# Scores, masks and shifts of an attention kernel as sixteen 32x32 tiles instead of four 32x128 tiles

## Chip, cores and metric

The kernel runs on one core of one Trainium2 chip. The metric is the device time of one execution in microseconds. The kernel before takes 2215.35 us, the median of three runs (2215.28 to 2217.46).

## The reference

Eight sequences of 1024 tokens with 512 features go through one gated attention layer, all in float32:

```
xn = layernorm(x)                                   # per token, no scale or offset
q, k, v = xn @ W.T + b                              # 16 heads of 32 features
scores  = q @ k.T / sqrt(32)                        # 1024 x 1024 per head
scores  = where(i % 256 >= j % 256, scores, -1e30)  # the mask repeats every 256
s   = softmax(scores) @ v @ Wo.T + bo
w   = +1 where weights >= 0 else -1
g   = silu(clip((xn @ w.T) * scale + bias, -100, 100))
out = x + s * g
```

## The kernel before, in words

**Order of the tokens.** Tokens are stored so that token `w * 256 + m` stands at place `4 * m + w`. The mask then depends on `m` alone, and a block of 128 places against a block of 128 places is either all kept, all masked (and left out), or on the diagonal, where a mask of 32 steps of 4 places is added.

**Sequences, groups, quads.** The main loop runs over 8 sequences `b`, 4 groups `g` of four heads, and 9 quads `n`: 288 steps. A quad is a PSUM tile of 128 partitions, 4 heads and 512 columns (one bank for each head). There is one quad buffer (`ps_q`, `bufs=1`), which two kinds of blocks use in turn:

- *Maxima* (`maxima_quad`, tile `s`, lines 513 and 525), for the group after the present one. Queries stand on the partitions, keys on the columns. Where the quad holds a diagonal block, a product of two bf16 constants (`place_of`, `after`, line 513) first puts the mask there. Then for each of the four heads a float32 product of 32 rows, the features of that head, adds the scores (line 525). VectorE takes the maximum over the keys (line 537).
- *Scores* (`probs_quad`, tile `t`, lines 592, 603 and 614), for the present group. Keys stand on the partitions, queries on the columns. First minus the maximum of each query is put on all 128 keys: a bf16 product of three rows, the three bf16 parts of the maximum, with a constant of -1 (line 592, `shift`). Then the mask (line 603) and the scores (line 614). ScalarE takes the exponential from the quad to SBUF (line 627).

The lists `S_QUADS` and `T_QUADS` say which blocks a quad holds: one segment of 512 columns, or two whose widths add up to 512 (128 and 384, or 256 and 256). Four of nine maxima quads and four of nine score quads have no mask.

**Tiles of TensorE.** A matmul uses as many rows of the array as its operands have partitions, and as many columns as its output has. In the quads each head's product is a tile of 32 rows and 128 columns (the shift: 3 rows of its 32), and the four heads lie side by side along the rows: `lhsT` and `rhs` start at partition `h * 32`, the output goes to the bank of head `h`. The names in the profile are 32*128 and 3*128. All other large products are tiles of 128 rows and 32 columns, four side by side along the columns: probabilities times values (`attend_quad`, line 640), the projections and the output (`product`, line 358), the sums of the probabilities (line 681) and the turn of the maxima (`shift_rows`, line 566). The gate (line 456) and the transposes (lines 259 and 328) use 128 by 128.

A float32 product is one instruction in the program and four on the engine: weight load, matmul, weight load, matmul. A bf16 product is one weight load and one matmul. So line 525 with one segment of 512 columns is 4 products, 8 matmuls, in two passes of four.

**What sets the order.** `tc.manual_schedule()` keeps the order in which the code issues. In each step it is: scores quad of this step (`probs_quad`), probabilities times values of the step before (`attend_quad`), a share of other work, the maxima quad of the next group (`maxima_quad`), and more other work. The other work (projections, gate, transposes, output) comes from a list for each group (`STEADY`, `OPENING`, `CLOSING`), where each piece has a cost written by hand; `fill` takes pieces until a wanted sum of costs is reached. The costs are constants in the code, not measured at run time.

## Time and profile before

| what | value |
|---|---|
| median of the runs | 2215.35 us |
| profiled execution, first to last instruction (span) | 2213.6 us |
| instructions in the span | 57362 |
| TensorE clock granted | 1.000 |
| DMA queues: instructions for TensorE (q8) | 203 packets, 3.33 MB |
| HBM read and written | 56.37 and 33.55 MB, 41 GB/s over the span |

The groups of the three kinds of quad work by shape (all four widths for the scores):

| line, shape | matmuls | mean ns of one | weight loads of the line, mean ns |
|---|---|---|---|
| 525 `s`, 32x512 float32 | 1536 | 632 | 184 |
| 614 `t`, 32x512 float32 | 1536 | 596 | 185 |
| 592 shift, 3x512 bf16 | 768 | 384 | 91 |
| 603 mask, 32x128 bf16 | 1024 | 215 | 93 |
| 513 mask, 32x256 bf16 | 384 | 278 | 91 |
| 640 `av`, 128x512 float32 | 1536 | 605 | 108 |

How to read it: the busy time of an engine is the union of its instructions' times, and matmuls that lie side by side overlap in it. Their ends are modelled. A mean of 632 ns is therefore not what a matmul takes from the engine; the distance between the starts of successive passes is. "PEld" are the weight loads, which run beside the matmuls. In a timeline, `x8` at the end of a line means that eight instructions were merged, and the second number is the time from the first start to the last end.

### The profile page before, as it was taken

How to read it: one execution, taken by the hardware profiler on the slowest of the kernel's cores; microseconds unless marked ns; L12 is line 12 of the kernel's file. 1: busy time of each engine (PE TensorE's matmuls, PEld its weight loads, DVE VectorE, ACT ScalarE, POOL GpSimd, SP SyncE). 2: the span in 40 equal slices, each digit the busy share in tenths (PEclk: the TensorE clock that was granted, in tenths of full speed). 3: DMA queues.
4: the chain of work that ended last, by engine and by line, in shares of the span. 5: the costliest groups of instructions: out<-in, count | busy, mean ns of one | idle time of the engine just before them, and what ended most of it. 6: DMA issues, size and time to landing. Idle time of an engine off the chain costs nothing. (4 is left out here: it accounts for less than half of the span.)

```text
span 2213.6 us, 57362 instructions
## 1 busy us (share of the span) xinstructions
PE 2182.9 (99%) x26015; PEld 857.3 (39%) x26015; DVE 1276.7 (58%) x1635; ACT 876.0 (40%) x862; POOL 1325.6 (60%) x1198
## 2 busy tenths in 40 slices
PE   8999999999999999999999999999999999999998
PEld 4334333333333443333333333334333443333333
DVE  4556556665557655566555665565655665555564
ACT  2235433444344444344443443434443343333332
POOL 1356565666566656576556665556765666755562
PEclk9999999999999999999999999999999999999999
DMA  4001000121001210012000120002200111000113
GB/s 167 2 16 35 11 7 30 54 73 35 25 25 40 73 35 25 25 59 72 16 25 25 63 68 16 25 25 68 63 16 25 45 59 63 11 21 25 44 54 125
DMA packets 49676, 93.60 MB, mean 42 GB/s; under 512 B 5388, under 2 KB 5656, under 8 KB 49432
## 3 DMA queue, kind: packets, MB, share of 16 engines
q1 hardware_dynamic: 48728, 88.76, 12.1%
q8 instruction: 203, 3.33, 0.6%
q10 hardware_dynamic: 704, 1.18, 0.2%
q14 instruction: 41, 0.34, 0.0%
HBM read 56.37 MB, written 33.55 MB: 41 GB/s over the span
## 5 line engine op out<-in xcount | busy, mean ns | idle before, releaser
L659 POOL TENSOR_TENSOR p<-p,p 128x512 f32<-128x512 f32 x930 | 1096.3, 1209 | 395.2 <-ACT p L627 242.9
L537 DVE TENSOR_REDUCE pm<-s 128x4 f32<-128x2048 f32 (+3 forms) x384 | 664.0, 1750 | 588.6 <-PE s L525 586.7
L627 ACT ACTIVATE p<-t 128x2048 f32<-128x2048 f32 x288 | 540.9, 1878 | 839.3 <-PE t L614 764.0
L715 DVE RECIPROCAL aT<-aT 128x128 f32<-128x128 f32 x256 | 230.3, 928 | 214.9 <-ACT aT L676 214.9
L525 PE MATMUL s<-k,q 32*128 32x512 f32 (+3 forms) x3072 | 315.3, 504 | 1.1 <-ACT q L401 0.8
L640 PE MATMUL av<-p,v 128*32 128x512 f32 (+3 forms) x3072 | 307.4, 495 | 1.6 <-DVE aT L719 1.4
L614 PE MATMUL t<-q,k 32*128 32x512 f32 (+3 forms) x3072 | 306.1, 492 | 0.0
L358 PE MATMUL k_ps<-xnT,wkT 128*32 128x512 f32 (+3 forms) x2832 | 254.9, 477 | 1.7 <-ACT wkT L274 0.7
L358 PE MATMUL q_ps<-xnT,wqT 128*32 128x512 f32 (+2 forms) x2656 | 254.1, 497 | 1.7 <-ACT shift L572 0.8
L358 PE MATMUL v_ps<-wvT,xnT 128*32 128x512 f32 (+3 forms) x2728 | 254.8, 489 | 0.0
L358 PE MATMUL o_ps<-woT,aT 128*32 128x320 f32 (+2 forms) x2568 | 243.9, 503 | 1.5 <-ACT shift L572 0.8
L741 POOL TENSOR_TENSOR s<-s,xb 128x512 f32<-128x512 f32 x63 | 86.3, 1370 | 212.3 <-DVE s L740 210.2
L358 PEld LDWEIGHTS k_ps<-xnT,wkT 128*32 128x32 f32 x2832 | 83.7, 109 | 169.0 <-issue 138.3
L614 PEld LDWEIGHTS t<-q,k 32*128 32x128 f32 x3072 | 139.1, 185 | 25.8
L358 PEld LDWEIGHTS q_ps<-xnT,wqT 128*32 128x32 f32 x2656 | 78.9, 109 | 174.0 <-issue 151.6
L640 PEld LDWEIGHTS av<-p,v 128*32 128x32 f32 x3072 | 70.3, 108 | 195.9 <-issue 163.4
L358 PEld LDWEIGHTS v_ps<-wvT,xnT 128*32 128x32 f32 x2728 | 79.2, 109 | 168.6 <-issue 143.5
L456 PE MATMUL y_ps<-fwT,x 128*128 128x512 f32 x464 | 135.5, 418 | 1.7 <-ACT k L401 1.3
L525 PEld LDWEIGHTS s<-k,q 32*128 32x128 f32 x3072 | 117.0, 184 | 52.0 <-ACT p L627 42.2
L358 PEld LDWEIGHTS o_ps<-woT,aT 128*32 128x32 f32 x2568 | 76.1, 109 | 151.4 <-issue 133.1
L429 POOL TENSOR_TENSOR x<-xnT,x 128x512 fp32r<-128x512 f32 x58 | 74.1, 1277 | 100.0 <-ACT x L428 100.0
L435 POOL TENSOR_SCALAR y<-y 128x512 f32<-128x512 f32 x64 | 39.6, 619 | 153.1 <-DVE y L434 101.3
(96 smaller groups left out, 1475.8 us busy)
## 6 DMA issues: line engine op xcount, KB each, us to landing
g<-t SPq DMA_DIRECT2D x64, 256.0 KB, 2.0
gb<-g SPq DMA_DIRECT2D x64, 256.0 KB, 2.9
xb<-in_L_attn_x_dram SPq DMA_DIRECT2D x64, 256.0 KB, 3.1
out_dram<-s SPq DMA_DIRECT2D x63, 256.0 KB, 2.5
x<-in_L_attn_x_dram SPq DMA_DIRECT2D x62, 256.0 KB, 3.1
wq_st<-in_L_attn_Wq_dram SPq DMA_DIRECT2D x2, 512.0 KB, 5.1
wv_st<-in_L_attn_Wv_dram SPq DMA_DIRECT2D x2, 512.0 KB
fw_st<-in_L_ffn_weights_dram SPq DMA_DIRECT2D x2, 512.0 KB, 9.7
```

Source lines behind the costliest of these rows:

```text
L358: nc.tensor.matmul(hold[0][cols, lo:hi], lhsT=lhsT[:, cols], rhs=rhs[:, lo:hi], start=(i == 0 and lo == 0), stop=(i == n - 1), skip_group_ ...
L429: nc.gpsimd.tensor_tensor(part[1], src, part[0].bitcast(F32), ALU.subtract)
L435: nc.gpsimd.tensor_scalar(y[0], y[0], MAX_VAL, -MAX_VAL, ALU.min, ALU.max)
L456: nc.tensor.matmul(hold[0], lhsT=part[i][:, c, :], rhs=wT["fw"][:, c, :], start=(i == 0 and c == 0), stop=(i == 1 and c == NC - 1),)
L525: nc.tensor.matmul(sc[:, h, at : at + w], lhsT=qt[b, g][head_rows(h), i * P : (i + 1) * P], rhs=kt[b, g][head_rows(h), lo:hi], start=(at = ...
L537: nc.vector.tensor_reduce(pm[:, 0 if lo == 0 else 1, i, :], sc[:, :, at : at + w], AX.X, ALU.max)
L614: nc.tensor.matmul(sc[:, h, at : at + w], lhsT=kt[b, g][head_rows(h), j * P : (j + 1) * P], rhs=qt[b, g][head_rows(h), q0 : q0 + w], start ...
L627: nc.scalar.activation(pt[:, :, :width], sc[:, :, :width], AF.Exp, scale=SCALE)
L640: nc.tensor.matmul(av[b, g, f][head_rows(h), lo : lo + w], lhsT=vt[b, j][:, g * P + h * DK : g * P + (h + 1) * DK], rhs=pts[b, g, n][:, h, ...
L659: nc.gpsimd.tensor_tensor(t[:, hs, lo : lo + w], t[:, hs, lo : lo + w], p[:, hs, at : at + w], ALU.add)
L715: nc.vector.reciprocal(r, r)
L741: nc.gpsimd.tensor_tensor(s, s, xr, ALU.add)
```

## The change

In `maxima_quad` and `probs_quad` every product of a head is split in four by its output partitions. `COLS` are the four slices of 32 columns of the array; each new product has 32 rows (3 in the shift) and 32 columns, takes 32 columns of `lhsT`, streams the same `rhs` as before, and writes 32 partitions of the head's bank. Heads are the outer loop, columns the inner one. Where there was a set of four products there is a set of sixteen. Operands, types, accumulation order and everything outside the two functions are as before.

```diff
+    COLS = [slice(c * DK, (c + 1) * DK) for c in range(NH)]
+    HEAD_COLS = [(h, c) for h in range(NH) for c in COLS]
...
                 rows_h = after[head_rows(h), :].unsqueeze(1)
-                nc.tensor.matmul(
-                    sc[:, h, :].rearrange("p (a t) -> p a t", t=P)[:, masked[0] :: step, :],
-                    lhsT=place_of[head_rows(h), :],
+                for c in COLS:
+                    nc.tensor.matmul(
+                        sc[c, h, :].rearrange("p (a t) -> p a t", t=P)[:, masked[0] :: step, :],
+                        lhsT=place_of[head_rows(h), c],
...
-            for h in range(NH):
+            for h, c in HEAD_COLS:
                 nc.tensor.matmul(
-                    sc[:, h, at : at + w],
-                    lhsT=qt[b, g][head_rows(h), i * P : (i + 1) * P],
+                    sc[c, h, at : at + w],
+                    lhsT=qt[b, g][head_rows(h), i * P + c.start : i * P + c.stop],
                     rhs=kt[b, g][head_rows(h), lo:hi],
...
-            for h in range(NH):
+            for h, c in HEAD_COLS:
                 r = slice(h * DK, h * DK + 3)
                 nc.tensor.matmul(
-                    sc[:, h, at : at + w],
-                    lhsT=neg1[r, :],
+                    sc[c, h, at : at + w],
+                    lhsT=neg1[r, c],
                     rhs=shift[b, g, f][r, lo : lo + w],
...
-                for h in range(NH):
+                for h, c in HEAD_COLS:
                     nc.tensor.matmul(
-                        sc[:, h, at : at + P],
-                        lhsT=after[head_rows(h), :],
+                        sc[c, h, at : at + P],
+                        lhsT=after[head_rows(h), c],
                         rhs=place_of[head_rows(h), :],
...
-            for h in range(NH):
+            for h, c in HEAD_COLS:
                 nc.tensor.matmul(
-                    sc[:, h, at : at + w],
-                    lhsT=kt[b, g][head_rows(h), j * P : (j + 1) * P],
+                    sc[c, h, at : at + w],
+                    lhsT=kt[b, g][head_rows(h), j * P + c.start : j * P + c.stop],
                     rhs=qt[b, g][head_rows(h), q0 : q0 + w],
```

More of the change, by code (lines that the diff above doesn't have):

```diff
@@ L512, in maxima_quad @@
                 rows_h = after[head_rows(h), :].unsqueeze(1)
-                nc.tensor.matmul(
-                    sc[:, h, :].rearrange("p (a t) -> p a t", t=P)[:, masked[0] :: step, :],
-                    lhsT=place_of[head_rows(h), :],
-                    rhs=rows_h.to_broadcast([MT, len(masked), P]),
-                    start=True,
-                    stop=False,
-                    skip_group_check=True,
-                )
+                for c in COLS:
+                    nc.tensor.matmul(
+                        sc[c, h, :].rearrange("p (a t) -> p a t", t=P)[:, masked[0] :: step, :],
+                        lhsT=place_of[head_rows(h), c],
+                        rhs=rows_h.to_broadcast([MT, len(masked), P]),
+                        start=True,
+                        stop=False,
+                        skip_group_check=True,
+                    )
         at = 0
```

## Prediction

> **What bounds the kernel now.** I read the page first. TensorE (PE) has work for 99% of the span at full clock, and no other engine passes 60%.

> ```profile
> PE 2182.9 (99%) x26015; PEld 857.3 (39%) x26015; DVE 1276.7 (58%) x1635; ACT 876.0 (40%) x862; POOL 1325.6 (60%) x1198
> ...
> PEclk9999999999999999999999999999999999999999
> ...
> q8 instruction: 203, 3.33, 0.6%
> ```

> The reader is to see that PE's own queue sets the end, that the clock hides nothing, and that 26015 matmuls and 26015 weight loads come in as 3.33 MB of instructions. Next I read the waits of PE alone, longest first:

> ```profile
> PE t L592 <- DVE pm L537: 4.2, 4, 1.5
> PE t L592 <- ACT p L627: 1.6, 5, 0.8
> ```

> These are the two longest, 5.8 us in all. PE waits for nobody, so whatever this change adds to or takes from PE goes straight into the time, and there is no cover. The diff touches no other engine: built, both programs have the same instructions in the same order on the other four queues, and the same waits and signals on PE.

> But a busy PE is not a PE at its peak, so the timeline comes third: not the durations, which are modelled and overlap, but the distance from one group's start to the next.

> ```profile
> 1000.58 0.40 PE L592 MATMUL t<-shift,neg 3*128 3x512 bf16 x4
> 1000.80 0.23 PE L603 MATMUL t<-place_of,after 32*128 32x128 bf16 x4
> 1000.86 1.08 PE L614 MATMUL t<-q,k 32*128 32x512 f32 x8
> 1001.88 1.07 PE L640 MATMUL av<-p,v 128*32 128x256 f32 x16
> 1002.76 1.05 PE L358 MATMUL k_ps<-xnT,wkT 128*32 128x192 f32 x16
> ```

> A float32 product runs as two passes, each of four matmuls side by side. av (1001.88 to 1002.76) streams 512 columns in two passes in 0.88 us; the scores (L614) need 1.02 us for the same. Where the maxima's scores have no mask in front it is worse:

> ```profile
> 1020.21 1.14 PE L525 MATMUL s<-k,q 32*128 32x512 f32 x8
> 1021.28 2.79 PE L358 MATMUL o_ps<-woT,aT 128*32 128x192 f32 x32
> ```

> That is 1.07 us. I therefore took the start of every PE instruction in the trace and subtracted the streaming time: 0.833 ns a column in float32, 0.417 in bf16, what steady runs show (128x32 passes of 512 columns repeat every 429 ns, a shift of 512 takes 0.22 us). Of 2207 us between PE starts 1940 is streaming; 267 is overhead. The 288 score blocks (T) and 288 maxima blocks (S) hold 580 us of streaming and 97.6 us of overhead inside them. Two things explain it:

> - *Leaving a tile size.* The last pass before another tile size lasts 107 ns longer after 32x128 tiles, 117 after 128x32, about 98 after a 128x128 transpose. Four tiles start one after the other, 3.6 ns apart with 32x128 and 6.6 ns with 128x32, so these are one number: 96 ns plus the lag of the last tile (3 x 3.6 = 11, 3 x 6.6 = 20).
> - *First weights.* Behind such a change the weights cannot be loaded early. The first pass then lasts 107 ns longer with 128 columns of float32 weights (S without mask), 27 with 32 columns (av). One mask pass in front hides about half of the 107.

> **The change, part by part.** In the built programs PE gains 4608 float32 products for each of L525 and L614 (two matmuls each), 4608 for the shift (L592), 3072 and 1920 for the masks (L603, L513). That is 18432 + 9600 = 28032 matmuls, and as many weight loads: 54047 of each after, 108094 instructions against 52030. The streamed columns stay: sixteen tiles stream at once where four did. That sixteen streams keep pace is not shown; four 128x32 tiles already cover the same 128 by 128 places, with a stream of their own each, at 429 ns a pass, so I cost it at nothing.

> 1. *First weights, less.* 32 columns to load instead of 128. Block overhead beyond the 107 of the exit, now and with 27 ns (13 for bf16, or behind a pass that covers the rest): S without mask 110 to 27, 128 blocks, 10.6 us; S with one mask 68 to 13, 64 blocks, 3.5; S in two segments 23 to 13, 96 blocks, 1.0; T with one mask 70 to 13, 64 blocks, 3.6; T in two segments 82 to 20, 96 blocks, 6.0; T without mask nothing. Sum: **-24.7 us**.
> 2. *Exit, more.* The last tile now lags by fifteen steps, not three. At 3.6 ns the exit is 96 + 54 = 150 (43 more), at 6.6 it is 96 + 99 = 195 (88 more). Times 576 blocks: +24.8 to +50.7 us. I take 6.6: twelve of fifteen steps go to another column of the array, and every row of the trace that does so has 6.6. **+50.7 us**.
> 3. *Narrow bf16 passes.* 384 passes (256 of masks in T, 64 in S, 64 of shifts) stream 128 columns in 53 ns and repeat every 57. Sixteen starts need 16 x 3.6 = 58 (nothing lost) or 16 x 6.6 = 106 (49 more each, 18.8 us). Same row, so **+18.8 us**.
> 4. *Feeding PE.* The trace has no long run as dense as the new blocks, so bounds. Below: nothing, if instructions come as fast as tiles start (3.3 ns each within a group now). Above: the densest 1000 starts of the trace took 33.4 us; if that were all PE can be fed, 108094 x 33.4 ns = 3610 us. The densest short runs are 32 starts in 0.22 us (7.0 each) and 64 in 0.69 us (10.8). Those are demands met, not limits, so I take **0** and keep the rest as a rival.

> Sum: -24.7 + 50.7 + 18.8 + 0 = +44.8 us on a span of 2213.6, 2258.4; the runs shown have 1.75 us more (median 2215.35), so **2260 us**. With 3.6 ns in 2 and 3 it would be +0.1, 2215: bounds 2215 to 2260 before item 4. What is late next is still PE; other engines' waits move with it. If the lag were covered (PE waiting elsewhere), items 2 and 3 would cost nothing, but only 5.8 us of such waits exist.

> [...] Matmuls on different tiles start 3.6 and 6.6 ns apart here. [...]

> **The rivals.**

> *A, the forecast*: only items 1 to 3 act, with a lag between 3.6 and 6.6 ns: 2205 to 2275. For it: the lag is visible at each group. Chance 0.45.

> *B, PE cannot be fed inside the blocks.* A T block in two segments would hold 256 instructions in 1.17 us, one each 4.6 ns, longer than any burst of the trace. At 7.0 ns: 96 such blocks lose 0.62 us each, 96 S blocks in two segments (160 instructions, 0.96 us) 0.16: 75 us, which with +44.8 gives 2335. At 10.8: 1.59 and 0.77 us each, 0.26 for 64 masked T, 0.13 for 64 masked S: 252 us, 2512. With the short lag the two are 2290 and 2467. Against it: PE shows no hole behind its densest bursts now. It decides from about 5 ns an instruction. I place it at 2275 to 2480, 0.31.

> *C, far slower*: PE is fed no faster than about 15 ns an instruction, or sixteen tiles stream as two sets of eight (580 us more). Up to 3610, 0.08.

> *D, the other side: no drain.* After the change every neighbour with 128x32 tiles has the same 32 columns. If PE drains only where the columns of a tile change, 479 entries (118 ns now) and 539 exits (107) fall to the 8 ns that a change of operands costs inside one tile size: 52.7 + 53.4 us, with item 1 another 24.7, so 2085; if only one side falls, about 2140; with a lag that eats part, up to 2205. Against it: 32x128 to 128x128 changes the rows alone and costs 105 ns. Chance 0.16.

> That the change does not do what it says is excluded by the built program.

> **How the numbers follow.** About 0.2% (4.4 us) is what a measurement of this kernel can tell from no change. A gives 0.06 faster (weights win, lag 3.6 or less), 0.08 same, 0.31 slower; B and C slower, D faster: 0.22 / 0.08 / 0.70. The range leaves out C (0.08) and the deeper part of D (0.11): 2170 to 2480. A alone: 2205 to 2275.

> **What would show it.** In the profile after: the same blocks, start to start. Item 1 is right if S without mask has a first pass near 454 ns instead of 534; item 2 if the last pass before another tile size is 150 to 195 longer than streaming; item 3 if mask passes repeat each 58 to 106 ns. B shows as holes between starts inside T blocks in two segments, where PE waits for nothing ("issue"), while plain S blocks stay good; D as exits near 8 ns. The instruction queue should carry about 6.9 MB. Wrong would be the whole sum if a float32 pass of sixteen tiles repeats at much more than 429 ns.

## The result, and the profile after

The changed kernel takes **2408.52 us**, the median of four runs (2407.01 to 2411.05); the kernel before, on the same chip, 2215.32 (2215.24 to 2217.46). The ratio is 1.0869, with a 95% interval of 1.0855 to 1.0883. The profiled execution has a span of 2406.3 us where the kernel before had 2213.6: +193. The forecast was 2260. The direction and the range held; of the size, 45 us out of 193 were foreseen.

The page of the changed kernel, by the lines that were read before:

```profile
PE 2374.5 (99%) x54047; PEld 977.2 (41%) x54047; DVE 1285.3 (53%) x1635; ACT 878.2 (36%) x862; POOL 1326.8 (55%) x1198
...
PEclk9999999999999999999999999999999999999999
...
q8 instruction: 422, 6.91, 1.2%
```

The work of the other engines is what it was (POOL 1326.8 us against 1325.6), the clock is full (1.0 granted), and the instruction queue carries the 6.91 MB that were expected. PE is "busy" for 99% here too, so this page alone does not say what it lost. The waits of PE don't either:

```profile
PE t L596 <- DVE pm L541: 3.1, 3, 1.3
PE xnT_ps L331 <- DVE x L315: 2.1, 2, 1.4
```

The longest is 3.1 us in total. But for such small sums PE still waits for nobody: the 193 us are its own. The timeline of PE shows where they are (start in us, time from the first start to the last end, line, operation, number of instructions):

```profile
1055.57 1.16 PE L529 MATMUL s<-k,q 32*32 32x512 f32 x32
1056.66 0.74 PE L361 MATMUL q_ps<-xnT,wqT 128*32 128x320 f32 x8
...
1059.38 0.43 PE L596 MATMUL t<-shift,neg 3*32 3x512 bf16 x16
1059.60 0.27 PE L607 MATMUL t<-place_of,after 32*32 32x128 bf16 x16
1059.79 1.29 PE L618 MATMUL t<-q,k 32*32 32x512 f32 x32
1061.01 1.06 PE L644 MATMUL av<-p,v 128*32 128x512 f32 x8
...
1067.45 0.44 PE L596 MATMUL t<-shift,neg 3*32 3x384 bf16 x32
1067.81 0.48 PE L607 MATMUL t<-place_of,after 32*32 32x128 bf16 x32
1068.08 1.49 PE L618 MATMUL t<-q,k 32*32 32x384 f32 x64
1069.50 1.07 PE L644 MATMUL av<-p,v 128*32 128x512 f32 x8
```

Take the distance from one start to the next. The maxima without mask (1055.57 to 1056.66) take 1.09 us, where they took 1.07. The scores with one mask (1059.38 to 1061.01) take 1.63, where they took 1.30: the shift keeps its 0.22, the mask takes 0.19 (was 0.06), the products 1.22 (was 1.02). The scores in two segments (1067.45 to 1069.50) take 2.05, where the kernel before takes 1.36 (1008.38 to 1009.74):

```profile
1008.38 0.40 PE L592 MATMUL t<-shift,neg 3*128 3x384 bf16 x8
1008.61 0.28 PE L603 MATMUL t<-place_of,after 32*128 32x128 bf16 x8
1008.72 1.09 PE L614 MATMUL t<-q,k 32*128 32x384 f32 x16
1009.74 0.64 PE L640 MATMUL av<-p,v 128*32 128x512 f32 x4
```

The same for all 576 blocks, with streaming subtracted as in the prediction. "Instructions" are weight loads and matmuls of PE in one block:

| block | number | instructions before, after | mean overhead before, ns | after, ns | difference, us |
|---|---|---|---|---|---|
| S, no mask | 128 | 16, 64 | 217 | 231 | +1.8 |
| S, one segment, mask | 64 | 24, 96 | 175 | 430 | +16.3 |
| S, two segments | 96 | 40, 160 | 130 | 634 | +48.4 |
| T, no mask | 128 | 24, 96 | 130 | 436 | +39.3 |
| T, one segment, mask | 64 | 32, 128 | 177 | 508 | +21.3 |
| T, two segments | 96 | 64, 256 | 188 | 871 | +65.6 |

Together that is 192.7 us, as much as the spans differ. One row stands apart: the block of 64 instructions is hardly slower, and every block of 96 or more is.

Inside a block the trace shows a stop. Here is the start of a score block without mask, cut off at 457.15 us:

```profile
456.88 0.44 PE L596 MATMUL t<-shift,neg 3*32 3x512 bf16 x16
457.09 0.62 PE L618 MATMUL t<-q,k 32*32 32x512 f32 x8
```

All sixteen tiles of the shift have started, but of the sixteen products only eight. Medians over the 128 blocks of this kind, in ns from the block's first start: the shift's tiles start at 0 to 50; the first eight products together at 226 to 250, as the shift ends; the ninth at 411, 185 ns after the first; the rest 16.7 ns apart until 528. The second pass repeats that stagger (first tiles at 659, last at 979), and the next group comes at 1496: the last tile's start, 427 of streaming, and 90. In the kernel before, such a block takes 1.18 us from start to start:

```profile
1024.00 0.39 PE L592 MATMUL t<-shift,neg 3*128 3x512 bf16 x4
1024.22 1.03 PE L614 MATMUL t<-q,k 32*128 32x512 f32 x8
1025.18 0.64 PE L640 MATMUL av<-p,v 128*32 128x512 f32 x4
```

### The profile page after: what moved, and what is told of

Its sections match the earlier page's. It is cut to its first block, busy times and chain, and to the rows that moved or that the text cites. A ratio compares the mean times of both kernels' runs of the same rounds, so it can differ in the third digit from the quotient of the medians.

```text
span 2406.3 us, 113426 instructions
## 1 busy us (share of the span) xinstructions
PE 2374.5 (99%) x54047; PEld 977.2 (41%) x54047; DVE 1285.3 (53%) x1635; ACT 878.2 (36%) x862; POOL 1326.8 (55%) x1198
## 3 DMA queue, kind: packets, MB, share of 16 engines
q8 instruction: 422, 6.91, 1.2%
q10 hardware_dynamic: 704, 1.18, 0.1%
## 5 line engine op out<-in xcount | busy, mean ns | idle before, releaser
L618 PE MATMUL t<-q,k 32*32 32x512 f32 (+2 forms) x12288 | 398.5, 489 | 0.5 <-issue 0.5
L529 PE MATMUL s<-k,q 32*32 32x512 f32 (+2 forms) x12288 | 381.7, 490 | 1.0 <-ACT q L404 0.8
L618 PEld LDWEIGHTS t<-q,k 32*32 32x32 f32 x12288 | 187.6, 103 | 39.2 <-issue 15.2
L529 PEld LDWEIGHTS s<-k,q 32*32 32x32 f32 x12288 | 145.3, 103 | 59.5 <-ACT p L631 39.7
```

The lines of the kernel that those rows point to most:

```text
L529: nc.tensor.matmul(sc[c, h, at : at + w], lhsT=qt[b, g][head_rows(h), i * P + c.start : i * P + c.stop], rhs=kt[b, g][head_rows(h), lo:hi] ...
L618: nc.tensor.matmul(sc[c, h, at : at + w], lhsT=kt[b, g][head_rows(h), j * P + c.start : j * P + c.stop], rhs=qt[b, g][head_rows(h), q0 : q ...
```

## Experiments

My theory after the result, **the queue**: PE takes in at most 64 instructions counted from the oldest that still streams. A bf16 tile is two of them, a float32 product four. A shift of sixteen tiles fills 32 places, eight products the other 32. Everything behind waits until the shift ends, then comes in at a rate of its own, and the exit waits for the last tile. Rivals: a **price for each instruction**, wherever it stands; the **fetch** of instructions from memory (q8); a limit on the number of **tiles or rows** that stream at once; the **tile size** itself.

### The order of the tiles

```diff
-    HEAD_COLS = [(h, c) for h in range(NH) for c in COLS]
+    HEAD_COLS = [(h, c) for c in COLS for h in range(NH)]
```

(and the same in the mask of the maxima)

> The changed kernel with the sixteen tiles of each set issued column by column (heads inside) instead of head by head. Queue theory (PE holds some 64 instructions ahead; those behind come at about 4.2 ns each, and after a full stop only some 185 ns later, so the second half of sixteen tiles starts late): the time stays, 2395 to 2415, and in T blocks the ninth tile still starts some 185 ns behind the eighth. If instead tiles of heads 3 and 4 are late because of their rows: the ninth tile is now head 1, so the gap goes from there, and about 0.2 us on each of 288 T blocks, to about 2350. My forecast's step that the lag of 6.6 ns belongs to a step between columns: with twelve of fifteen steps now between heads the lag in S blocks without mask falls to about 4 ns a tile, some 40 ns on 128 blocks, 5 us.

Measured: 2408.43 us, ratio 1.0868 (1.085 to 1.0886). Every row of the table is as in the changed kernel, the ninth tile is still the late one, and the tiles of the maxima still start 6.7 ns apart. So it isn't a matter of which rows or columns come next. It also takes down the reason that I gave for item 2: 6.6 ns don't belong to a step to another column.

### Sixteen tiles only where the block has 64 instructions

```diff
-            for h, c in HEAD_COLS:            # maxima
+            for h, c in WHOLE if masked else SPLIT:
```

(all else in 32x128 tiles, as in the kernel before)

> The kernel before with 32x32 tiles only in the four maxima quads without a mask (128 blocks, 6144 more PE instructions); all else in 32x128. Queue theory: these 64 instructions fit into what PE holds ahead, so each block goes from 217 ns of overhead to about 231 as in the changed kernel: 2 us more, 2217. Rival, a price for each added PE instruction wherever it stands (193 us over 56064 instructions, 3.44 ns): 21 us more, 2236.

Measured: 2221.5 us, 1.0024 (1.0014 to 1.0035), some 4 above what the queue theory expected and 15 below the price for each instruction. A price for each instruction is refuted: 128 blocks with four times the instructions cost 1.8 us more inside them, as the queue theory has it. Another 3.4 us came where it had nothing, at the starts of score blocks; see below, "Where the rest went".

### Half as many, larger tiles

```diff
-    COLS = [slice(c * DK, (c + 1) * DK) for c in range(NH)]
+    COLS = [slice(c * 64, (c + 1) * 64) for c in range(2)]
```

> The changed kernel with two tiles of 64 columns for each head, eight side by side (18688 more PE instructions than before). Queue theory: 32 instructions for 512 columns of scores, so only two-segment blocks (80 to 128 instructions) run past 64; first weights of 64 columns cost 54 ns instead of 107, the exit has seven steps of lag: 2205 to 2225. Rival, a price per added instruction: 18688 x 3.44 ns = 64 us more, 2279.

Measured: 2235.27 us, 1.0087 (1.0072 to 1.0102), 10 above what I expected at most. Inside the blocks +14.4 us over the kernel before: score blocks in two segments, 128 instructions, cost 310 ns of overhead where they cost 188; some with 64 or fewer are better than before (194 against 217 in S without mask, 32 instructions; 150 against 177 in T with one mask, 64). T without mask, with 48 instructions, is 27 ns worse: staying under 64 does not make a split free. The other 6.8 us are at the starts of blocks, as in the last one.

### The same number of products, not the same tiles

```diff
-            for h in range(NH):
-                nc.tensor.matmul(sc[:, h, at : at + w], ...)
+            for c in range(0, w, P):
+                for h in range(NH):
+                    nc.tensor.matmul(sc[:, h, at + c : at + c + P], ...)
```

(against the kernel before: tiles of 32x128, each product cut along the streamed columns)

> The kernel before, tiles 32x128 as there, but each float32 product of 512 columns issued as up to four products of 128 streamed columns: 36864 more PE instructions, the count that the changed kernel adds for the scores, without sixteen tiles. Queue theory: four tiles repeat every 107 ns with 16 instructions, some 6.7 ns each, and the queue holds the next groups, so 0 to 20 us more, 2215 to 2235. Rival, a price per added instruction: 127 us more, 2342.

Measured: 2234.84 us, 1.0082 (1.0067 to 1.0097). As many float32 products as after in each one-segment block, but a piece streams a quarter as long and, by the queue theory, gives its places back early: 150 ns of overhead (median) in T without mask, where the changed kernel has 429. Again the number of instructions is not the price.

### Without shift and masks

```diff
-                nc.tensor.matmul(sc[c, h, at : at + w], lhsT=neg1[r, c], ...)      # shift
-                    nc.tensor.matmul(sc[c, h, at : at + P], lhsT=after[...], ...)  # masks
-        nc.scalar.activation(pt, sc, AF.Exp, scale=SCALE)
+        nc.scalar.activation(pt, sc, AF.Exp, scale=1e-4)
```

> The changed kernel without the masks and without the shift by the maximum (the exponential takes the raw scores times 0.0001): only the float32 scores are left in both kinds of quads, as 32x32 tiles. To be read against its twin in 32x128. Queue theory: 384 one-segment blocks have what S without mask has now (231 against 217 ns of overhead), two-segment blocks of 128 instructions run past the queue: twin plus 20 to 70 us, about 2200. Rival, a price per added instruction: 36864 x 3.44 ns, twin plus 127 us.

> The twin: the kernel before without the masks and without the shift, in 32x128 tiles. From the blocks of before: 89 us of streaming gone, 29 us more of first weights that nothing covers any more: about 2156 by both theories.

Measured: 2245.04 us with sixteen tiles, 2158.76 with four: +86, above the 20 to 70 that I expected. Where I had a number for a block, it held: one segment, now 64 instructions, costs 230 ns (four tiles: 218). A score block of the first kernel, by the timeline of PE:

```profile
1053.06 1.15 PE L577 MATMUL t<-q,k 32*32 32x512 f32 x32
1054.14 1.07 PE L603 MATMUL av<-p,v 128*32 128x512 f32 x8
```

1.08 us from start to start, and no stop among the 32 matmuls. The sixteen tiles are the same as in the changed kernel; only the 32 instructions of the shift in front are gone, and with them 200 ns of overhead. Two segments, 128 instructions, cost 572 ns against 225: that is where my estimate was low (96 + 96 blocks, 67 us in all), and another 14 us are at the starts of blocks.

### How fast PE can be fed, alone

The layer is left out; TensorE alone issues sixteen 32x32 tiles again and again:

```
for _ in range(64):
    for h in range(4):
        for c in S32:
            matmul(sc[c, h, 0:64], lhsT=h16[S32[h], c], rhs=h16[S32[h], 0:64])
```

> PE alone: stretches of matmuls that need nothing from other engines, each behind five full 128x128 float32 products so that the queue is full at its start; the layer itself is left out, the output is a copy of x. Queue theory: 32x32 bf16 of 64 columns runs at 8.3 ns a pair after the first 64 instructions, for as long as it lasts (2048 instructions, 8.5 us), 32x128 bf16 of 64 columns is bound by its streaming (27 ns for four pairs) or the same 8.3 ns a pair (33 ns). If the fetch of instructions by DMA were the limit, a long stretch would slow down after a few hundred instructions, and its packets (256 instructions) would follow each other without a gap; packets of the changed kernel take 1.0 us, 3.9 ns an instruction, so this would show here at the latest. Float32 32x32 of 512 columns in a row: 427 to 440 ns a pass for sixteen tiles; much more would mean that sixteen streams hinder each other.

Measured: the first 32 matmuls, 64 instructions with their loads, start 3.3 ns apart; then comes a gap of 121 to 123 ns; then one matmul with its load each 8.3 ns, 4.17 ns an instruction. So far as expected. But it doesn't last for the 8.5 us that I expected: after some 200 matmuls each 128 of them, which is 256 instructions, are followed by a stop of 2.4 us or more. The busy times by window show what that comes to (columns: window, length, PE busy and its matmuls, weight loads busy and their number, two engines that do nothing, granted clock, DMA share, GB/s):

```profile
10.00:65.00 55.00, 10.27 (x1014) 8.93 (x1014) 0.00 (x0) 0.00 (x0) 0.54 0.77 250
71.70:98.80 27.10, 10.03 (x1025) 8.88 (x1024) 0.00 (x0) 0.00 (x0) 0.58 0.02 4
```

The second row is the undisturbed one: 1025 matmuls in 27.1 us, 26 ns each, or 13 ns an instruction. (In the first, the copy of the input loads the DMA queues.) One packet of the instruction queue (256 instructions: in the changed kernel 422 packets bring 108094) then arrives every 3.3 to 4.3 us. That is a second and slower limit, for long stretches. For the changed kernel it is no bound: its packets come every 5.27 us in the median, 62 of 422 in less than 4 us, and the overhead of a kind of block hardly varies, which it would if the fetch were late here and there. I put it at an estimated 1 to 2 us of the 193: the waits of PE that the profile marks "issue" come to 1.4 us in the changed kernel and to none in the kernel before. No run separates it.

The same run has sixteen float32 tiles of 512 columns six times in a row, 64 instructions a set. The first four passes begin at 0, 453, 882 and 1311 ns, so sixteen tiles stream side by side in the 429 ns that four take. From the third set on the stops are back: the sets then begin 1041 to 1055 ns apart, where two passes of 429 would be 858. With eight 32x64 tiles, 32 instructions a set, passes repeat each 429 ns after the first.

### The tiles counted

TensorE alone again: n bf16 tiles of 512 columns, then n float32 products of 512 columns on the same tiles, with 128x128 matmuls between the repeats:

```
for h, c in TILES[0:n]:
    matmul(sc[c, h, 0:512], lhsT=h16[S32[h], c], rhs=h16[S32[h], 0:512])
for h, c in TILES[0:n]:
    matmul(sc[c, h, 0:512], lhsT=f[S32[h], c], rhs=f[S32[h], 0:512])
```

> PE alone, blocks built like a score quad without a mask (a bf16 pass of 512 columns, then float32 products of 512), but with 4, 8, 9, 10, 12 or 16 tiles, each block six times behind 128x128 products that let the queue fill; then 8 tiles in the rows of the third and fourth head, then 16 without the bf16 pass; the layer is left out, the output is a copy of x. Queue theory in its sharper form, that PE takes in at most 64 instructions counted from the oldest one that is still streaming: two for each tile of the bf16 pass and four for each float32 product, so 4 to 10 tiles (24 to 60 instructions) start their float32 products without a gap, with 12 the eleventh and with 16 the ninth starts about 185 ns behind the one before, and 16 without the bf16 pass have no gap. If eight tiles are the limit whatever stands ahead: a gap already with 9 and 10. If the rows of heads 3 and 4 are slow: a gap with the second set of 8.

With ten tiles, then with twelve and sixteen, then sixteen without the bf16 pass:

```profile
141.94 0.41 PE L138 MATMUL quad<-h 32*32 32x512 bf16 x10
142.16 1.05 PE L140 MATMUL quad<-f 32*32 32x512 f32 x20
143.14 0.70 PE L113 MATMUL wide<-f 128*128 128x512 f32 x1
```

```profile
171.17 0.42 PE L144 MATMUL quad<-h 32*32 32x512 bf16 x12
171.40 1.24 PE L146 MATMUL quad<-f 32*32 32x512 f32 x24
172.57 4.56 PE L113 MATMUL wide<-f 128*128 128x512 f32 x10
...
182.95 0.43 PE L150 MATMUL quad<-h 32*32 32x512 bf16 x16
183.17 1.34 PE L152 MATMUL quad<-f 32*32 32x512 f32 x32
184.44 4.56 PE L113 MATMUL wide<-f 128*128 128x512 f32 x10
```

```profile
252.97 1.14 PE L162 MATMUL quad<-f 32*32 32x512 f32 x32
254.04 4.56 PE L113 MATMUL wide<-f 128*128 128x512 f32 x10
```

From the first float32 start to the next group: 0.98 us with ten tiles, 1.17 with twelve, 1.27 with sixteen, 1.07 with sixteen and nothing in front. The starts inside say it in full. With 4, 8, 9 and 10 tiles all products start 3.3 ns apart. With 12, the eleventh starts at 185 ns. With 16, the ninth does, and the rest follow 16.7 ns apart. Twelve bf16 tiles are 24 instructions and ten products 40; sixteen are 32 and eight products 32; ten are 20 and 40, and all go in. Each time the line falls at **64**. A limit of eight tiles falls with the ten that start at once, a limit by rows with eight tiles on the rows of the two other heads, which show no stop. One thing the runs can't tell apart: every matmul here has a weight load of its own, so 64 instructions and 32 matmuls with their loads are the same count.

### Sixteen tiles for the scores, four for shift and masks

```diff
+    HEAD_WHOLE = [(h, slice(0, P)) for h in range(NH)]
-            for h, c in HEAD_COLS:            # shift, masks
+            for h, c in HEAD_WHOLE:
```

> The changed kernel with shift and masks back in 32x128 tiles, the scores alone in 32x32: 19200 PE instructions fewer, but 448 more changes of tile size, of columns alone, inside blocks. Queue theory with about 107 ns for each such change: T without mask 231 + 107 = 338 (now 436), T with mask 338 (508), T in two segments 679 (870), S with mask 338 (430), S in two segments 679 (634): 43 us less than the changed kernel, 2365. Rival D of the forecast in another form, that a change of columns alone costs nothing: 48 us less again, 2317. Price per instruction: 66 us less than the changed kernel, 2342.

Measured: 2383.01 us, 1.0754 (1.074 to 1.0769). Inside the blocks it is near what was expected, kind by kind, by medians: 331 and 682 ns in S with a mask (expected 338 and 679), 330, 334 and 692 in T (338, 338, 679); together 43 us less than in the changed kernel. The saving of places in the queue is partly eaten by the change from 32x128 to 32x32 inside a block, which costs about 100 ns although only the columns differ (330 ns in T without mask, against 231 for the same float32 products with nothing in front, S without mask of the changed kernel). So a drain does not hang on the rows alone. Rival D, that it hangs on the columns alone, falls with the changed kernel, where the tiles on both sides differ in their rows alone and the exit still takes 90 ns. The total is 18 us above the expected 2365, none of it inside the blocks.

### A mixture by the rule of 64

```diff
+        cols = TWO if len(S_QUADS[n]) == 1 else ONE                                     # maxima
+        cols = TWO if len(segs) == 1 and segs[0][1] * P >= segs[0][0] * HALF else ONE   # scores
```

(`TWO` are two slices of 64 columns, `ONE` is the whole 128: 32x64 only where the third run showed a gain)

> 32x64 tiles where the run with 32x64 everywhere had a smaller block overhead than before, 32x128 elsewhere: one-segment maxima quads (194 against 217 ns without mask, 170 against 175 with), one-segment score quads with a mask (150 against 177). From those blocks: -2.9, -0.3 and -1.7 us, 4.9 us less than before, 2210 to 2211; score quads that wait for VectorE's maxima may gain up to 2 us more. Rival, a price per added PE instruction (4096 + 3072 + 4096 or so times 3.44 ns): 30 to 40 us more than before.

Measured: 2214.49 us, 0.9992 (0.9983 to 1.0001) against the kernel before: no difference that can be told. The blocks gave 5.3 us, where 4.9 were expected (217 to 192 ns in S without mask, 175 to 170 and, in T, 177 to 150 with one mask); 4.2 us went again at the starts of other blocks, so the total misses the expected 2210 to 2211. It beats the changed kernel by 194 us and equals the kernel before.

### Where the rest went

Five runs have microseconds at the *starts* of blocks that none of my theories had. Each block reuses the one quad buffer, so it waits for the engine that read the last quad: S for ScalarE's exponential, T for VectorE's maximum. I compared each of the 576 starts with the same one of the kernel before, and with the end of that engine's instruction. Of what the run with four tiles for shift and masks lost there, 9.1 us lie in the 126 S blocks that begin within 100 ns of the exponential's end and 4.5 in the 61 T blocks within 100 ns of the maximum's; all others together, under 0.4. A place in that run's timeline, with PE, ScalarE and the weight loads:

```profile
452.30 1.08 PE L646 MATMUL av<-p,v 128*32 128x512 f32 x8
452.62 1.88 ACT L633 ACTIVATE p<-t 128x2048 f32<-128x2048 f32 x1 [5.37 <-PE t L620]
...
454.55 0.24 PEld L531 LDWEIGHTS s<-k,q 32*32 32x32 f32 x32 [0.36 <-ACT p L633]
```

and the same in the changed kernel:

```profile
1053.39 1.07 PE L644 MATMUL av<-p,v 128*32 128x512 f32 x8
1053.56 1.88 ACT L631 ACTIVATE p<-t 128x2048 f32<-128x2048 f32 x1 [4.75 <-PE t L618]
...
1055.57 0.25 PEld L529 LDWEIGHTS s<-k,q 32*32 32x32 f32 x32 [0.30 <-ACT p L631]
```

The exponential takes 1.88 us in both, but it begins 0.32 us after PE has gone on to av in the first, and 0.17 in the second. The weight load that waits comes 0.05 us behind its end in the first and 0.13 in the second, where nothing was late. By medians: in the score quads 1 to 4 ScalarE starts 215 to 228 ns after PE's next group behind four 32x128 tiles, 337 to 338 behind sixteen whose last pass starts 6.7 ns apart (the run above), and 188 to 189 behind sixteen that run out of the queue (the changed kernel). VectorE, in the maxima quads 4 and 7, has 145, 257 and 108. PE's other work between two quads is measured out so closely that 110 ns of delay become a wait. One of the nine S quads has nothing to spare even in the kernel before: it begins 53 ns (median) after the exponential's end, as the load that waits does above. The list of PE's waits has no row for it, because it is the weight loads that wait: the idle time of those of `s` that the page puts down to ScalarE is 49.1 us in that run and 42.2 in the kernel before. That the later start of the readers is the cause is my reading of these starts; no run changes it alone. The same count explains the bare kernel (9.6 + 5.4 us), the 32x64 tiles (4.0 + 2.8), the mixture (1.6 + 2.6) and the maxima alone (3.4). In the changed kernel itself it is nearly nothing (starts of blocks 71.4 us, before 73.1).

## Why the prediction was right and wrong

**The bound, right.** PE waits for next to nothing, before and after, and the difference lies in the blocks that the diff touches.

**Item 4, "Feeding PE", is the step that failed.** I took 0 out of bounds of 0 to 3610 us, because the dense rows were "demands met, not limits". That is no reason for either end. The limit that these runs show is no rate but a number: 64 instructions, weight loads and matmuls both counted, from the oldest that streams (32 and 32 with sixteen tiles, 24 and 40 with twelve), then a stop of 185 ns, then 4.17 ns an instruction. With the other items as sized, it cost 148 us (193 less 44.8). Counted by blocks: those of 96 instructions or more took 191 us longer, where items 1 to 3 gave them 44. The prediction counted 256 and 160 instructions for two kinds of blocks in rival B, and put them against a rate, not against 64; a block without mask in T, 96 instructions, was not counted at all, and is 39 us of the 193.

**Rival B** is what happened, inside the range of 2275 to 2480 that I gave it, between its sums by 7.0 and by 10.8 ns. Its sign came as it said: stops inside T blocks in two segments with no wait shown, plain S blocks nearly as before. But its mechanism, a fixed time for each instruction, is refuted by the second and the fourth run; that 2408 lies between its ends is luck.

**Item 1, right where it can be seen.** In S without mask everything ahead of the last pass is 10.2 us shorter (forecast 10.6), in S with one mask 2.8 (forecast 3.5). Elsewhere the stop covers it.

**Item 2, right mechanism, wrong reason, and a size that holds for one kind.** The exit is a constant and the last tile's lag: from the end of the last tile's streaming to the next group 90 ns in every kind, before and after. In S without mask the lag is 114 ns in the mean (forecast 99): 13 steps of 6.7 and two of some 15. That makes +12.0 us for 128 blocks where 11.3 were forecast. But 6.7 ns is not what a step to another column takes: in the other order it is the same, and products that wait ready in the queue start 3.3 ns apart. The trace of the kernel before had it already: its four 32x128 tiles in S without mask, which differ in their rows alone, start at 0, 7, 13 and 20 ns, against the 3.6 ns a step that I read for that size. Where the queue ran out, the lag of the last tile is 184 ns in T with two segments and 273 to 344 in the other kinds (medians).

**Item 3, wrong both ways.** Where the queue is full, in T with two segments, the masks repeat each 134 ns (sixteen times 8.33, two instructions each), above the 106 that I gave as the most. Where it is not, in S with one mask, the sixteen start 3.3 ns apart and the first product follows at 66 ns, as it does behind four tiles: nothing is lost.

**Rival D** is refuted: the drain stays at 90 ns although nearly all neighbours have 32 columns too. **Rival C**: PE can be fed as slowly as 13 ns an instruction, but only over stretches longer than these blocks; sixteen tiles do stream at once, in 429 ns a pass.

**The steps from start to start.** In the changed kernel tiles start 3.3 and 6.7 ns apart up to 64 instructions, and a float32 product each 16.7 ns beyond. The run with TensorE alone has 8.3 ns for a matmul with its load in short stretches and 26 in long ones.

**Open.** What the 185 ns are made of, and what sets 4.17 ns, no run shows. Nor does one show why ScalarE and VectorE learn of sixteen tiles that end close together some 110 ns later, though in both traces, before and after, only the last matmul of each of the 576 blocks carries a signal.

## What to carry to other kernels

Before splitting a matmul into smaller tiles, count instructions (a float32 product is four, a bf16 one two) from the oldest that still streams to the last of the group: up to 64 the split costs little here (14 ns a block in S without mask, 27 in T without mask as 32x64), beyond that the rest starts late (185 ns), and the next change of tile size waits for the last of them (90 ns from the end of its streaming). A resource whose limit no row shows should not be put at nothing because all demands so far were met; put the count of the new demand beside every figure at hand, a depth as well as a rate. And a version that saves on PE pays only if the engines that hand the buffer back are not the next to be late (in the run with four tiles for shift and masks 9.1 and 4.5 us went at such starts).
